# Turning x and B for a Mamba scan: transposing DMAs with GpSimd copies in place of TensorE transposes

## The chip, the cores and the metric

The kernel runs on one core of one Trainium2 chip. The metric is device time in microseconds, from the first to the last instruction of the launch and what lies around them; the median of three runs before the change is 1356.73 us (1356.61 to 1357.14).

The core has a matmul engine (TensorE, PE in the profile, its weight loads PEld), VectorE (DVE), ScalarE (ACT), GpSimd (POOL) and SyncE (SP), which here issues all DMAs.

## What is computed

A Mamba-2 layer, a residual sum with a layer norm, then a feed-forward layer with ternary weights and a second residual sum with a layer norm. The input is 2 sequences of 2048 tokens, 512 wide, in float32. Of the reference, the part that the change touches:

```python
zxbcdt = jnp.einsum('bld,ed->ble', u, W_in)
...
for k in range(D_CONV):
    xconv = xconv + xp[:, k:k + l, :] * conv_w[:, k]
xBC = jax.nn.silu(xconv)
x = xBC[..., :D_INNER].reshape(b, l, NHEADS, D_HEAD)
Bm = xBC[..., D_INNER:D_INNER + NGROUPS * D_STATE]
Cm = xBC[..., D_INNER + NGROUPS * D_STATE:]
...
Y_diag = jnp.einsum('bcshn,bczhn,bchsz,bczhp->bcshp', Ch, Bh, Lmat, xdt)
states = jnp.einsum('bczhn,bchz,bczhp->bchpn', Bh, decay_states, xdt)
...
Y_off = jnp.einsum('bcshn,bchpn,bchs->bcshp', Ch, prev_states, jnp.exp(cum))
y = (Y_diag + Y_off).reshape(b, l, h, p)
```

There are 8 heads of 128, one group of B and C with 64 states, and a state carried along each sequence.

## The kernel before

**Tiling and stages.** The first part goes over 16 groups of 256 tokens (`TG`), each of two chunks of 128 (`NC` = 2). `proj(g)` multiplies u (held as two float16 parts) by W_in: six pieces for z (L754) and nine blocks of 128 channels for x, B and C (L779), channels on partitions, tokens along the row. Block 8 holds B and C. On each block ScalarE applies one tap of the convolution as it reads PSUM (L792), VectorE the other three (L794), and ScalarE the silu (L798 for x, L809 and L811 for B and C).

The scan needs x and B with tokens on partitions. So TensorE transposes each block's two chunks of 128x128 float32 against `ident` into the PSUM bank `tr` (L802), and ScalarE copies the result into `xt` (L804). B's two pieces of 64x128 go the same way (L815, L817) into `bt`.

`steps(g)` computes dt and its running sum. The sum goes through DRAM (`cum_scratch`), so that it comes back as rows spread over all partitions (`cr`, `ec`; L873, L887), and VectorE subtracts and clips (L878). `scan(g, c)` handles one chunk: B^T C (L916) into the PSUM bank `ms`, masked (L917); the state's part of y (L930); the state's update, from B weighted (L934) and `xt` (L941, L948); the decay times dt times B^T C (L956) plus D on the diagonal (L958), multiplied by `xt` (L963); the gate (L965). Then a norm: a sum of squares (L970), a power on GpSimd (L972), and y in two float16 parts `yh` (L973) and `yl` (L975), which transposing DMAs turn into `th` and `tl` (L974, L976) for the output product with W_out (L983). ScalarE takes it out of PSUM (L986), and a DMA stores it in DRAM (L987).

Beside the groups the feed-forward weights are read, turned into ternary values (L1025 to L1027) and combined (L1032). The second part goes over 8 blocks of 512 tokens: a layer norm, seven products in place of eight for each of the three matrices (L1096, L1148), and the closing norm. It transposes its input by DMA too, as two float16 parts staged in `stg` (L1229).

**Order.** Every piece of work is an `op` of `Order`, with its engine, a cost, what it reads and writes, and a key from the list `KEYS`. `Order.run` goes through a planned time: on each engine it takes the ready `op` with the smallest key for which buffers are free, hands out the buffers and charges the `op`'s cost to its own engine alone. The order so found is emitted, and each engine then runs its own list strictly in that order; SP's list is its DMA queue, and an entry that waits holds up those behind it. GpSimd's list holds only small powers (L636, L696, L972, L1206, L1254) after the set-up.

**Buffers.** `tr` is one bank of PSUM, `ms` another. `xc` has four places of 256 columns, `xt` two of a whole group. `S` and `stg` (two of 2 KB each) and `us0` serve the feed-forward part alone. In `steps`, `scan` and the feed-forward part nothing but the names of this section is touched.

Of the kernel before, what the change touches and what calls it, by code (L numbers as in the profile page):

```python
# [12 lines left out]
F8 = mybir.dt.float8e4  # L13
AF = mybir.ActivationFunctionType
# [27 lines left out]
140 139 245 183 268 349 233 268 348 194 134 321 296 448 210 232 291 190 119 151 181 177 348 247 218 261 115 305 164  # L42
156 191 164 299 171 402 237 384 367 385 734 917 930 182 172 214 387 415 409 155 325 203 200 94 160 411 337 214 337
306 163 337 337 398 327 152 395 396 161 424 399 370 532 576 542 630 514 661 622 639 762 564 135 134 239 197 239 175
264 316 219 65 355 279 384 295 420 283 449 508 614 674 694 896 928 938 689 786 668 873 896 964 889 1242 891 879 920
999 856 952 1038 862 772 996 138 22 76 34 102 42 112 114 329 138 130 112 99 188 298 84 176 176 107 -9 160 159 116
228 128 172 210 252 211 348 304 268 316 448 420 282 390 703 399 394 474 429 430 431 395 523 337 463 372 462 456 506
687 744 752 824 727 794 786 782 88 348 349 169 216 212 185 465 437 664 529 411 520 533 514 508 544 572 535 552 573
594 574 575 512 592 592 684 540 600 745 640 687 606 625 698 681 289 225 340 448 309 142 340 370 436 348 176 190 353
303 273 175 379 282 662 640 695 696 597 682 778 667 200 316 294 129 255 19 205 231 602 626 650 607 735 517 783 670  # L50
369 283 422 447 626 339 450 353 549 385 632 679 549 255 600 642 617 779 763 660 708 652 712 701 264 514 514 538 827
520 575 638 528 653 736 692 226 314 489 471 146 173 56 172 214 182 117 630 408 305 608 674 535 671 685 738 681 720
717 1085 685 717 932 870 877 900 873 849 862 891 839 950 947 1129 940 946 975 1019 997 898 913 1088 936 1171 1438
989 989 1139 1105 997 437 344 217 489 494 615 643 593 586 512 384 223 402 421 480 368 470 638 782 725 786 797 739
827 999 1068 421 391 426 397 406 450 807 777 511 453 602 559 538 638 675 710 1142 1095 1194 1098 1113 1034 1154 1228
940 1055 950 984 1020 1098 1229 1360 984 1048 1193 967 973 1187 1224 1086 531 551 671 557 576 776 937 1032 889 894
1312 1249 1199 1067 797 830 563 573 764 795 790 827 876 878 839 1007 748 903 912 1329 1056 1066 1158 1072 981 1141
998 1103 1170 1206 1444 1395 529 563 797 869 796 778 793 855 882 844 861 839 924 829 830 913 924 908 912 980 935 949
1046 1060 993 1059 1066 966 1272 193 389 496 575 873 572 615 680 629 1188 938 1028 916 1051 1133 1161 872 1133 1225
1078 1364 1222 1382 1412 1405 1415 1480 1388 1472 1405 1454 1474 1368 1476 1560 1475 1499 1564 1415 1338 1504 1438  # L60
1394 1526 1636 1374 1214 1537 1818 1314 767 595 684 789 809 880 893 748 1006 1054 796 718 816 838 802 984 1082 1249
979 789 988 1060 920 1363 1338 1294 701 655 707 599 719 875 1052 986 836 875 884 954 973 1184 1031 1013 1034 1078
1065 1107 1189 1229 1079 1122 1066 1215 1085 1215 857 1204 1355 1433 1172 1198 1018 1265 1347 1277 1356 1530 614 658
733 656 649 699 835 939 1324 1361 928 872 1286 1397 1030 1049 949 1047 1156 1374 1354 1024 1410 1321 1413 1070 1400
1305 1414 1269 1291 1285 1291 1295 1478 1156 1426 1215 1403 1303 1441 1446 1439 1769 1394 866 991 1300 1389 1379
1436 1406 1368 1637 1239 1522 1397 1289 1278 1546 1392 1528 1790 1537 1618 1612 1259 1635 1357 1711 1648 1599 1996
1848 1240 1288 1412 1359 1425 1235 1428 1557 1445 1443 1380 1334 1574 1479 1520 1614 1624 1640 1871 1749 1972 2068
1842 1771 1752 1797 1815 1863 1829 1704 1917 1920 1807 1989 1852 2037 1664 2336 1769 1954 1996 1986 1920 1827 1994
1818 1746 1933 1887 1822 869 1331 1482 1499 1511 1601 1522 1496 1478 1709 1313 1514 1516 1516 1491 1564 1435 1675
1495 1702 1559 1609 1538 1847 1635 1608 1536 1737 1709 1709 1623 1827 1750 1929 1552 1749 1700 1656 1692 1974 1869  # L70
1918 1759 1949 1877 1875 1983 1875 1701 1913 1402 1735 1613 1553 1580 1673 1541 1764 1317 1624 1590 1516 1496 1614
1510 1621 1455 1699 1581 1324 1524 1689 1665 1798 2011 1967 1689 1808 1909 1873 1660 1905 1251 1309 1632 1626 1716
1572 1437 1581 1772 1690 1692 1665 1740 1664 1697 1679 1789 1550 1792 1718 1811 1747 1919 2171 1754 1870 1861 2146
2078 1142 1229 1681 1732 1920 1867 1880 1546 2129 1933 1964 1802 1940 1784 1812 1705 1962 2095 2094 1878 1958 1936
2031 1906 1961 2109 2118 1986 2525 1816 1668 1775 1706 1694 1981 1786 1974 1838 2093 1857 1906 2115 1910 2020 1866
1984 2047 2155 1960 2107 1921 2179 2123 1998 2150 2055 2086 2121 2075 2026 2123 1953 2053 2077 1979 2079 2327 2178
2162 2282 2376 2291 2472 2482 2308 2258 2103 2339 2344 1886 1735 1754 1933 1963 1960 1829 1888 2162 2209 1782 2008
2008 2049 1977 2311 2168 2061 1973 2081 1936 1949 1795 2227 2141 2162 1805 1998 2012 1797 1874 2141 1970 2023 1830
1908 1695 1888 1973 2186 1990 1932 2122 2067 2181 2052 2123 1999 2130 2127 1685 2023 1776 1892 1799 1900 1884 2028
2122 2253 2334 2339 2329 2055 2330 2304 1960 2014 1954 1918 1998 2119 2112 1971 2099 1992 2257 2154 2144 2273 2191  # L80
2156 1483 1637 1927 2118 2183 2206 2115 2057 1942 2171 2120 2216 2359 2036 2147 2040 2086 2181 2341 2192 2259 2268
2310 2489 2266 2369 2526 2438 2489 1689 1833 2030 2182 2257 2240 2194 2247 2498 2251 2150 2213 2309 2141 2170 2164
2351 2370 2327 2539 2485 2355 2460 2421 2457 2462 2448 2606 2785 2328 2087 2227 2195 2202 2320 2285 2305 2421 2198
2239 2384 2272 2296 2412 2263 2332 2203 2645 2223 2450 2405 2616 2457 2539 2774 2490 2613 2502 2585 2673 2676 2732
2752 2541 2462 2657 2714 2693 2933 2749 2911 2908 2518 2768 2820 2995 2645 2771 2889 2355 2276 2340 2475 2361 2370
2531 2413 2605 2533 2411 2199 2395 2619 2460 2468 2543 2587 2264 2325 2494 2403 2293 2455 2375 2488 2610 2488 2604
2680 2552 2614 2716 3088 2659 2488 2624 2622 2570 2876 2729 2797 2398 2445 2620 2354 2452 2575 2626 2697 2374 2577
2420 2458 2490 2316 2674 2906 2869 2734 2332 2532 2477 2752 2583 2749 2664 2615 2632 2681 2642 2874 2764 2925 3149
3124 3048 3154 3124 3092 3076 2931 1999 2139 2305 2593 2611 2521 2384 2454 2587 2474 2539 2681 2547 2479 2616 2516
2465 2692 2555 2745 2690 2694 2678 2803 2696 2873 2817 2764 3052 2216 2399 2423 2687 2704 2561 2711 2688 2895 2630  # L90
2598 2527 2807 2618 2560 2590 2549 2890 2726 2957 3025 3119 2945 2875 2907 2947 2915 3215 3424 2205 2544 2494 2403
2242 2393 2370 2730 2358 2828 2878 2725 2800 2911 2557 2863 2467 2834 2956 2899 3018 2820 2684 2608 2702 2797 2723
2784 2875 2884 3020 2942 2983 2915 2994 2938 3056 3163 3100 3053 3057 3280 3118 3484 3444 3266 3320 3221 3341 3430
3163 3101 2969 3134 3139 3269 3211 3132 3262 3338 2760 2710 2599 2661 2539 2813 3129 3048 3083 3125 2898 2982 2836
3056 3043 3099 2978 3118 2762 2775 2693 3117 3110 3184 2756 2965 2546 2636 2733 3367 3087 3195 2698 2895 2586 2635
2631 3039 3099 3136 3164 3232 3074 3254 3142 3341 3190 3293 3103 3068 3288 3069 3062 3095 3132 3112 2518 2457 2752
2477 2558 2722 3017 2999 2682 3140 3249 3245 3217 3137 3071 3016 2785 2599 2669 2780 2747 3099 2615 3052 3037 2827
2860 3068 3101 2745 2769 3080 3044 3166 3125 3060 3222 3235 3300 3265 3337 3297 3324 3464 3418 2672 2432 3081 2834
2916 3185 3134 3233 3384 3161 3160 3284 3280 2867 3017 3196 3213 3407 3280 3289 3365 3338 3394 3319 3419 3437 3421
# [225 lines left out]
class Slot:  # L325
# [5 lines left out]
    def view(self, shape, dtype):  # L331
        n = 1
        for s in shape[1:]:
            n *= s
        size = n * (1 if dtype == F8 else 2 if dtype == F16 else 4)
        assert size <= self.hi - self.lo
        a = self.tile[:shape[0], self.lo // 4:(self.lo + size) // 4]
        if dtype != F32:
# [973 lines left out]
```

## Time and profile before

| | us |
|---|---|
| median of three runs | 1356.73 |
| span of the profiled execution | 1355.1 |
| ACT evictions of x's transposes (L804), 128 | 47.9 busy, 374 ns each |
| ACT evictions of B's transposes (L817), 16 | 266 ns each (median) |
| PE transposes of x (L802), 256 | 50.2 busy, 278 ns each |
| PE products B^T C (L916), 64 records for 32 products | 15.3 busy |
| DVE taps (L794), 432 | 480 ns each (median) |
| POOL power for the norm (L972), 32 | 548 ns each (median) |
| SP transposing DMAs `th`, `tl` (L974, L976), 64 | 3.2 and 3.3 from issue to landing |
| SP transposing DMAs of the second part (L1229), 56 | 3.1 from issue to landing |

A float32 product is recorded as two matmuls where the program has one of them. "Busy" is the union of the instructions' spans; ends of matmuls are modelled and overlap the next one's start. "Idle before" in a group's line is the time for which the engine stood still just ahead of these instructions, and the name behind an arrow is what ended it. The last x transpose (L802) starts 732.9 us into the span, the last product that reads `xt` (L963) at 745.3, and the last output eviction of the first part (L986) at 766.2. The granted clock of TensorE is 0.998.

### The profile page before, as it was taken

What the parts mean: (1) busy time and instruction counts of PE and PEld (TensorE: products, weight loads), DVE (VectorE), ACT (ScalarE), POOL (GpSimd) and SP (SyncE); (2) the same over time, 40 slices, a digit from 0 to 9 for tenths busy, and PEclk for the clock granted to TensorE, in tenths of its full rate; (3) what the DMA queues carried; (4) which work ended last, traced back from release to release, by engine and by line L of the source; (5) the groups of instructions that cost most, each with busy time, mean ns of one, the idle gap of its engine ahead of it and who ended that gap; (6) DMA issues with size and microseconds to landing.
All of it is one profiled execution on the core that took longest, in us unless ns stands there. A gap on an engine that the chain in (4) does not pass through costs nothing.

```text
span 1355.1 us, 28913 instructions
## 1 busy us (share of the span) xinstructions
PE 1334.2 (98%) x11024; PEld 1057.9 (78%) x11024; DVE 1143.1 (84%) x3070; ACT 1041.0 (77%) x1996; POOL 80.4 (6%) x127
## 2 busy tenths in 40 slices
PE   9999999999999999999999999999999999999997
PEld 7777667766776677777676788888888888888886
DVE  5988878878999889889888697987979797979985
ACT  8888777768788778787767695969778695959772
POOL 1000000000000010000000000101010100001000
PEclk9999999999999999999999999999999999999999
DMA  6445666534543553573439530413222231314101
GB/s 242 139 116 147 171 164 165 147 111 124 155 137 99 156 139 80 137 185 85 112 76 247 127 63 9 125 24 110 40 79 55 94 56 60 82 40 102 32 17 47
DMA packets 194811, 145.60 MB, mean 107 GB/s; under 512 B 140656, under 2 KB 151920, under 8 KB 194672
## 3 DMA queue, kind: packets, MB, share of 16 engines
q1 hardware_dynamic: 194672, 143.75, 40.7%
q8 instruction: 86, 1.41, 0.4%
q14 instruction: 53, 0.43, 0.1%
HBM read 89.84 MB, written 22.41 MB: 83 GB/s over the span
## 4 chain that ended last, share of the span: by engine, by line
PE 66%; DVE 17%; ACT 10%; DMA 4%; issue 2%; POOL 0%; SPq 0%; POOLq 0%; ACTq 0%; DVEq 0%
PE sd L1096 9%; PE mm L779 9%; PE po L983 8%; PE mm L754 8%; PE po L1148 5%; PE sd L1148 4%; PE mm L1096 3%; PE po L1096 3%; PE sd L963 3%; DVE acc L794 3%; PE ms L1148 2%; DVE cr L956 2%; PE ms L1096 2%; PE mm L1148 2%; PE tr L802 2%
## 5 line engine op out<-in xcount | busy, mean ns | idle before, releaser
L1096 PEld LDWEIGHTS <-wx 128*128 128x128 fp8e4 x2048 | 200.2, 98 | 27.3 <-issue 2.9
L794 DVE SCALAR_TENSOR_TENSOR acc<-mm,cwu,acc 128x256 f32<-128x256 f32 x405 | 189.3, 479 | 21.6 <-ACT acc L792 19.2
L779 PEld LDWEIGHTS <-wx 128*128 128x128 f16 x1620 | 155.6, 97 | 33.2 <-issue 1.1
L1096 PEld LDWEIGHTS <-wz 128*128 128x128 fp8e4 x1536 | 150.2, 98 | 22.8 <-issue 4.6
L779 PE MATMUL mm<-uh,wx 128*128 128x260 f16 x1080 | 142.8, 274 | 0.7 <-DVE acc L794 0.5
L754 PE MATMUL mm<-wz,uh 128*128 128x344 f16 x720 | 119.9, 309 | 2.5 <-DVE acc L794 1.4
L983 PE MATMUL po<-wo,th 128*128 128x512 f16 x512 | 121.0, 379 | 0.3 <-ACT js L986 0.3
L792 ACT ACTIVATE acc<-mm,cst,cwu 128x256 f32<-128x256 f32 x135 | 74.8, 556 | 33.3 <-PE mm L779 31.8
L754 PEld LDWEIGHTS <-uh 128*128 128x128 f16 x720 | 68.5, 98 | 37.5 <-issue 4.4
L983 PEld LDWEIGHTS <-th 128*128 128x128 f16 x512 | 49.0, 98 | 49.5 <-issue 1.2
L779 PE MATMUL mm<-ul,wx 128*128 128x260 f16 x540 | 82.1, 273 | 0.0
L768 ACT ACTIVATE sz<-mm,szs 128x344 f32<-128x344 f32 (+1 forms) x90 | 48.4, 539 | 33.1 <-PE mm L754 28.4
L956 DVE SCALAR_TENSOR_TENSOR cr<-cr,dt,gm 128x128 f32<-128x128 f32 x256 | 72.1, 347 | 0.3
L798 ACT ACTIVATE xc<-acc 128x256 f32<-128x256 f32 x128 | 52.3, 412 | 25.5 <-DVE acc L794 25.1
L754 PE MATMUL mm<-wz,ul 128*128 128x344 f16 x360 | 67.2, 309 | 0.0
L963 PE MATMUL sd<-xt,cr 128*128 128x128 f32 x512 | 66.5, 277 | 0.1
L963 PEld LDWEIGHTS sd<-xt,cr 128*128 128x128 f32 x512 | 62.0, 192 | 3.1 <-issue 0.7
L983 PE MATMUL po<-wo,tl 128*128 128x512 f16 x256 | 60.5, 379 | 0.0
L878 DVE TENSOR_SCALAR cr<-cr,cum 128x128 f32<-128x128 f32 x256 | 54.0, 281 | 6.6 <-DMA cr<-cum_scratch 6.6
L804 ACT ACTIVATE xt<-tr 128x256 f32<-128x256 f32 x128 | 47.9, 374 | 11.7 <-PE tr L802 10.7
L1148 PEld LDWEIGHTS <-xt 128*128 128x128 f16 x512 | 50.1, 98 | 6.6 <-DVE xt L1131 0.9
L802 PE MATMUL tr<-ident,xc 128*128 128x128 f32 x256 | 50.2, 278 | 0.2
(356 smaller groups left out, 3275.1 us busy)
## 6 DMA issues: line engine op xcount, KB each, us to landing
cr<-cum_scratch SPq DMA_DIRECT2D x32, 512.0 KB, 5.6
ec<-cum_scratch SPq DMA_DIRECT2D x64, 128.0 KB, 5.5
fraw<-in_wupT_dram SPq DMA_DIRECT2D x32, 256.0 KB, 3.4
s_scratch<-js SPq DMA_DIRECT2D x32, 256.0 KB, 2.3
x<-s_scratch SPq DMA_DIRECT2D x32, 256.0 KB, 3.1
fraw<-in_wgateT_dram SPq DMA_DIRECT2D x32, 256.0 KB, 3.1
fraw<-in_wdownT_dram SPq DMA_DIRECT2D x32, 256.0 KB, 3.1
uraw<-in_uT_dram SPq DMA_DIRECT2D x15, 520.0 KB, 3.8
```

What stands on the lines that cost most here:

```text
L754: T.matmul(ps[:, :ZC], (uh, ul)[a][:, k, HL + c * P:HL + (c + 1) * P], wz4[b]()[:, j, k, :], start=(n == 0), stop=(n == 11))
L779: T.matmul(ps[:, :TW], wx4[a]()[:, j, k, :], (uh, ul)[b][:, k, :], start=(n == 0), stop=(n == 11))
L792: op(f"t{j}3", "S", act(TG, 2), lambda: S.activation(acc.ap, ps[:, HL:TW], AF.Identity, bias=cb[:, j:j + 1], scale=tap(3)), r=[ps, kc] + k ...
L794: op(f"t{j}{k}", "V", stt(TG), lambda k=k: V.scalar_tensor_tensor(acc.ap, ps[:, 1 + k:1 + k + TG], tap(k), acc.ap, ALU.mult, ALU.add), r=[ ...
L798: op(f"xs{j}", "S", silu(TG), lambda: S.activation(xc.ap, acc.ap, AF.Silu), r=[acc], w=[xc], table="silu")
L802: T.transpose(tr[:, c * P:(c + 1) * P], xc[:, c * P:(c + 1) * P], ident)
L878: V.tensor_scalar(cr[:, h, :], cr[:, h, :], cum[:, c * NH + h:c * NH + h + 1], 0.0, ALU.subtract, ALU.min)
L956: V.scalar_tensor_tensor(cr[:, h, :], cr[:, h, :], dt[:, c, h:h + 1], gm.ap, ALU.mult, ALU.mult)
L963: T.matmul(yp[hf][:, i * P:(i + 1) * P], cr[:, h, :], xt[:, c, h, :], start=is_first(g, c), stop=(is_first(g, c) or i == 3))
L983: T.matmul(po.ap, t[:, k, :], wo3[b]()[:, k, :], start=(q == 0 and k == 0), stop=(q == 2 and k == 7))
L1096: T.matmul(bank_[:, fi * TG:(fi + 1) * TG], wt[:, kt, f * P:(f + 1) * P], xT[i][:, a, :, kt, :], start=(first and fi == 0 and n == 0), sto ...
L1148: T.matmul(bank_[:, s_ * TG:(s_ + 1) * TG], X[k][j][:, a, e, s_ * P:(s_ + 1) * P], wt[:, k, :], start=(first and s_ == 0 and k == 0 and a ...
```

## The change

x and B are no longer turned by TensorE. ScalarE writes the silu of two neighbouring blocks into one `xc` (128 x 2 x 256 float32). GpSimd copies it as 16-bit words into `xst`, with all lower halves first and all upper halves behind them (`xi`, 2048 half words a partition). One transposing DMA turns the eight 128x128 tiles of half words into `xtt` (`xT`), and a second GpSimd copy joins the halves into float32 in `xt` (`xo`). A group has four of each. `xt` is now ordered by head, then chunk.

B is written by two activations, chunk 0 on partitions 0 to 63 and chunk 1 on 64 to 127, and goes the same way with 512 half words (`bi`, `bT`, `bo`), once a group. B^T C of both chunks is issued as one `op` of two products, whose operands lie on the two halves of the partitions, into two banks: `ms` takes over the bank `tr`.

The new staging buffers lie where `S`, `stg` and `us0` of the feed-forward part lie. Over the kernel TensorE has 288 transposes fewer, ScalarE 144 evictions fewer and 16 activations more, GpSimd 160 copies more, and SP 80 transposing DMAs more. All keys are new, and are read in hundredths instead of tenths, so the order of all work is another one, in the feed-forward part too. The planner's cost for a copy on GpSimd is `GC`.

```diff
--- before.py
+++ after.py
@@ -11,6 +11,7 @@
 F8 = mybir.dt.float8e4
+U16 = mybir.dt.uint16
 AF = mybir.ActivationFunctionType
...
 KEYS = """
-140 139 245 183 268 349 233 268 348 194 134 321 296 448 210 232 291 190 119 151 181 177 348 247 218 261 115 305 164
...
+-30479 132366 121996 -139138 53213 144054 145003 115337 159198 104723 -139139 129284 102640 122916 9708 125093
...
 """
@@ -332,7 +406,7 @@
...
-        size = n * (1 if dtype == F8 else 2 if dtype == F16 else 4)
+        size = n * (1 if dtype == F8 else 2 if dtype in (F16, U16) else 4)
@@ -409,7 +483,7 @@
...
-            o.key = int(k) / 10
+            o.key = int(k) / 100
@@ -586,9 +660,9 @@
...
-        for name, size, bufs in (("acc", 1024, 4), ("xc", 1024, 4), ("gq", 4096, 2)):
+        for name, size, bufs in (("acc", 1024, 4), ("xc", 2048, 2), ("gq", 4096, 2)):
             room(name, size, bufs, True)
-        for name, rest, parts in (("wo", 2048, (("wo", 8192, 2),)), ("BC", 0, (("B", 1024, 2), ("C", 1024, 2)))):
+        for name, rest, parts in (("wo", 2048, (("wo", 8192, 2),)), ("BC", 1024, (("B", 512, 2), ("C", 1024, 2)))):
@@ -598,10 +672,16 @@
...
-        for name, size, bufs in (("x1", 8192, 2), ("us0", 2048, 1), ("S", 2048, 2), ("stg", 2048, 2)):
-            room(name, size, bufs)
+        room("x1", 8192, 2)
+        room("us0", 2048, 1)
+        for name, first, size, bufs in (("S", "xst", 2048, 2), ("stg", "xtt", 2048, 2)):
+            host[name] = [pool.tile([P, size // 4], F32, name=f"{name}_{i}") for i in range(bufs)]
+            for nm in (first, name):
+                od.tag(nm, [Slot(t, 0, size) for t in host[name]])
+        for i, nm in enumerate(("bst", "btt")):
+            od.tag(nm, [Slot(host["us0"][0], (2 * i + k) * 512, 512) for k in range(2)])
         bank = [psum.tile([P, DM], F32, name=n) for n in ("mm0", "mm1", "tr", "sd0", "sd1", "sd2", "ms", "po")]
-        for name, bs in (("mm", (0, 1)), ("tr", (2,)), ("mx", (3, 4)), ("sd", (3, 4, 5)), ("ms", (6,)), ("po", (7,)),
+        for name, bs in (("mm", (0, 1)), ("mx", (3, 4)), ("sd", (3, 4, 5)), ("ms", (6, 2)), ("po", (7,)),
@@ -610,7 +690,7 @@
...
-                room(tag, size * (2 if dtype == F16 else 4), 2)
+                room(tag, size * (2 if dtype in (F16, U16) else 4), 2)
@@ -625,6 +705,7 @@
...
+        GC = lambda n: 0.15 + n * 1.9 / 1200.0
@@ -792,34 +873,36 @@
...
-                tr = mk("tr", [P, DM])
                 if j < 8:
-                    xc = mk("xc", [P, TG])
-                    op(f"xs{j}", "S", silu(TG), lambda: S.activation(xc.ap, acc.ap, AF.Silu), r=[acc], w=[xc], table="silu")
-
-                    def xtr():
-                        for c in range(NC):
-                            T.transpose(tr[:, c * P:(c + 1) * P], xc[:, c * P:(c + 1) * P], ident)
-                    op(f"xt{j}", "PE", 0.22, xtr, r=[xc], w=[tr])
-                    op(f"xe{j}", "S", act(TG), lambda: S.activation(d["xt"][:, :, j, :], tr[:, :TG].rearrange("p (c w) -> p c w", c=NC), AF.Copy), r=[tr], w=[(d["xt"], j)])
+                    if j % 2 == 0:
+                        d["xc"] = mk("xc", [P, 2, TG])
+                    xc, jp = d["xc"], j // 2
+                    op(f"xs{j}", "S", silu(TG), lambda: S.activation(xc[:, j % 2, :], acc.ap, AF.Silu), r=[acc], w=[(xc, j % 2)], table="silu")
+                    if j % 2:
+                        st, tt_, xt = mk("xst", [P, 2, 2 * TG], U16), mk("xtt", [P, 2, 2 * TG], U16), d["xt"]
+                        op(f"xi{jp}", "G", GC(4 * TG), lambda: G.tensor_copy(st.ap, xc.ap.rearrange("p j n -> p (j n)").bitcast(U16).rearrange("p (n e) -> p e n", e=2)), r=[xc], w=[st])
+                        op(f"xT{jp}", "SP", 1.25, lambda: nc.sync.dma_start_transpose(
+                            out=tt_.ap.rearrange("p e (r q) -> p (e r) q", q=P), in_=st.ap.rearrange("p e n -> p (e n)")), r=[st], w=[tt_], kb=330)
+                        op(f"xo{jp}", "G", GC(4 * TG), lambda: G.tensor_copy(
+                            xt[:, 2 * jp:2 * jp + 2].rearrange("p j c q -> p (j c q)").bitcast(U16).rearrange("p (n e) -> p e n", e=2), tt_.ap), r=[tt_], w=[(xt, jp)])
                 else:
-                    B = d["B"] = mk("B", [64, TG])
+                    B = d["B"] = mk("B", [P, P])
...
-                    op("bs", "S", 0.42, lambda: S.activation(B.ap, acc[0:64, :], AF.Silu), r=[acc], w=[B], table="silu")
+                    for c in range(NC):
+                        op(f"bs{c}", "S", silu(P), lambda c=c: S.activation(B[c * 64:c * 64 + 64, :], acc[0:64, c * P:(c + 1) * P], AF.Silu), r=[acc], w=[(B, c)], table="silu")
...
-
-                    def btr():
-                        for c in range(NC):
-                            T.transpose(tr[:, c * 64:(c + 1) * 64], B[:, c * P:(c + 1) * P], ident[:64, :64])
-                    op("btr", "PE", 0.25, btr, r=[B], w=[tr])
-                    op("bte", "S", act(P), lambda: S.activation(bt.ap, tr[:, :P].rearrange("p (c w) -> p c w", c=NC), AF.Copy), r=[tr], w=[bt])
+                    bst, btt = mk("bst", [P, 2, P], U16), mk("btt", [P, 2, P], U16)
+                    op("bi", "G", GC(TG), lambda: G.tensor_copy(bst.ap, B.ap.bitcast(U16).rearrange("p (n e) -> p e n", e=2)), r=[B], w=[bst])
+                    op("bT", "SP", 1.25, lambda: nc.sync.dma_start_transpose(out=btt.ap, in_=bst.ap.rearrange("p e n -> p (e n)")), r=[bst], w=[btt], kb=100)
+                    op("bo", "G", GC(TG), lambda: G.tensor_copy(
+                        bt.ap.rearrange("p c n -> p (c n)").bitcast(U16).rearrange("p (n e) -> p e n", e=2), btt.ap), r=[btt], w=[bt])
...
-            d["xt"] = mk("xt", [P, NC, NH, P])
+            d["xt"] = mk("xt", [P, NH, NC, P])
@@ -911,9 +994,14 @@
...
-            gps = mk("ms", [P, DM])
-            gm = mk("gm", [P, P])
-            o("gps", "PE", 0.45, lambda: T.matmul(gps[:, :P], B[:, cs], C[0:64, cs], start=True, stop=True), r=[B, C], w=[gps])
+            if c == 0:
+                d["gps"] = [mk("ms", [P, DM]) for _ in range(NC)]
+
+                def gmm(gp=d["gps"]):
+                    for i in range(NC):
+                        T.matmul(gp[i][:, :P], B[rows(i), :], C[rows(i), i * P:(i + 1) * P], start=True, stop=True)
+                o("gps", "PE", 0.5, gmm, r=[B, C], w=d["gps"])
+            gps, gm = d["gps"][c], mk("gm", [P, P])
@@ -938,7 +1026,7 @@
...
-                            T.matmul(sp[rows(hf), i * P:(i + 1) * P], bw[:, hf * 4 + i, :], xt[:, c, hf * 4 + i, :], start=True, stop=True)
+                            T.matmul(sp[rows(hf), i * P:(i + 1) * P], bw[:, hf * 4 + i, :], xt[:, hf * 4 + i, c, :], start=True, stop=True)
@@ -960,7 +1048,7 @@
...
-                        T.matmul(yp[hf][:, i * P:(i + 1) * P], cr[:, h, :], xt[:, c, h, :], start=is_first(g, c), stop=(is_first(g, c) or i == 3))
+                        T.matmul(yp[hf][:, i * P:(i + 1) * P], cr[:, h, :], xt[:, h, c, :], start=is_first(g, c), stop=(is_first(g, c) or i == 3))
...
```

## The prediction

> **What bounds the kernel now.** I read first the page's busy times and the chain of waits, then the stage in which the edit lies, then TensorE's timeline around one transpose.
>
> ```profile
> PE 1334.2 (98%) x11024; PEld 1057.9 (78%) x11024; DVE 1143.1 (84%) x3070; ACT 1041.0 (77%) x1996; POOL 80.4 (6%) x127
> PE 66%; DVE 17%; ACT 10%; DMA 4%; issue 2%; POOL 0%; SPq 0%; POOLq 0%; ACTq 0%; DVEq 0%
> ```
>
> TensorE is nearly full, and the chain lies on it for two thirds; VectorE comes second in both. Next, busy time by stage (columns: stretch, PE, PEld, DVE, ACT, POOL, clock, DMA share, GB/s): the middle of the first part, and the feed-forward part, whose instructions the edit leaves as they are.
>
> ```profile
> 92.00:690.00 598.00, 594.51 (x4604) 423.75 (x4604) 510.96 (x1633) 466.04 (x889) 27.26 (x39) 1.00 0.52 136
> 736.00:1355.00 619.00, 605.99 (x5480) 534.50 (x5479) 516.22 (x1070) 459.28 (x880) 41.28 (x62) 1.00 0.28 67
> ```
>
> In the first part VectorE is busy 510.96/598 = 85.4%, and TensorE hardly idles. One group's length: the second output eviction (L986) of group 0 starts at 115.7, that of group 15 at 766.2, so (766.2 - 115.7)/15 = 43.4 us. VectorE works 0.854 x 43.4 = 37.1 us of it and has 6.3 to spare.
>
> A busy TensorE row overstates one short instruction, since ends are modelled. Start to start tells what a transpose takes from the stream:
>
> ```profile
> 301.78 0.75 PE L754 MATMUL mm<-wz,ul 128*128 128x344 f16 x4
> 302.36 0.38 PE L802 MATMUL tr<-ident,xc 128*128 128x128 f32 x2
> 302.58 1.06 PE L779 MATMUL mm<-uh,wx 128*128 128x260 f16 x8
> ```
>
> The pair takes 302.58 - 302.36 = 0.22 us, not 0.38; over all 128 pairs the median is 0.218.
>
> **What is removed.** TensorE: 128 pairs for x at 0.218 = 27.9 us, and 16 pairs for B at 0.238 (the same reading, L815) = 3.8. B^T C (L916) stands now as two products, 0.11 to 0.21 apart start to start; as a pair on separate row halves one may hide behind the other: 16 x 0.11 to 0.21 = 1.8 to 3.4, of which I take 2.3. Together 34 us in 16 groups, 2.1 a group: 41.3 us if TensorE goes on setting the pace. ScalarE loses 128 evictions of 0.374 and 16 of 0.266, 52 us, and gains 16 activations (one for B becomes two). It stands at 77% and not on the path, so I count nothing; if its cover fails that is a gain already limited by TensorE.
>
> **What is added to GpSimd.** 128 copies of 2048 half words a partition and 32 of 512. No such copy is in this trace. The nearest rows:
>
> ```profile
> masks.py:199 POOL TENSOR_SCALAR_AFFINE_SELECT ident<-ident 128x128 f32<-128x128 f32 x1 | 0.3, 292 | 0.1
> masks.py:197 POOL MEMSET ident<- 128x128 f32 x1 | 0.2, 204 | 0.3 <-POOLq L1302 0.3
> L1302 POOL MEMSET const-bfloat16-1.0<- 128x1 bf16 x1 | 0.1, 102 | 0.0
> ```
>
> From one element to 128 the memset grows by 102 ns, 0.80 ns an element; the affine select, if it starts from the same 102, by 1.50. So the large copy takes 1.75 to 3.16 us and the small one 0.51 to 0.87. A copy has no arithmetic and is nearest to the memset: I take 1.75 and 0.51. A group then has 8 x 1.75 + 2 x 0.51 = 15.0 us of copies, and GpSimd is free for that (27 us busy in 598).
>
> **What the copies do to VectorE** decides the case. GpSimd's small powers show that the two engines get in each other's way. Alone a power takes 0.55 us:
>
> ```profile
> 165.96 0.69 DVE L925 TENSOR_TENSOR ec<-ec,BC 128x512 f32<-128x512 f32 x1
> 166.05 1.00 POOL L636 TENSOR_TENSOR iu<-sc,half 128x1 f32<-128x1 f32 x1 [24.03 <-DVE q L850]
> ...
> 505.83 1.28 DVE L975 SCALAR_TENSOR_TENSOR yl<-y,rs,yh 128x1024 f16<-128x1024 f32 x1
> 505.99 1.52 POOL L636 TENSOR_TENSOR iu<-sc,half 128x1 f32<-128x1 f32 x1 [4.65 <-DVE sc L635]
> ...
> 240.62 0.55 POOL L636 TENSOR_TENSOR iu<-sc,half 128x1 f32<-128x1 f32 x1 [12.89 <-DVE dec L924]
> 240.66 0.70 DVE L925 TENSOR_TENSOR ec<-ec,BC 128x512 f32<-128x512 f32 x1
> ```
>
> Where a VectorE instruction with two SBUF inputs was already running, the power ended 0.40 us after that instruction's end (166.65 to 167.05; 507.11 to 507.51): GpSimd waited for all of it. Beside instructions that read PSUM (L794, L965) powers kept 0.55. In the third pair the power came first, and VectorE lost at most 0.01 us; but a power reads one element, a copy 2048. So the bounds of what a copy takes from VectorE are nothing, and all of the copy's time in which a two-SBUF instruction is due. I take the second, because in the one direction that the rows show the wait is for the whole instruction.
>
> How often one is due: instructions with two SBUF inputs (L956, L958, L975, L925, L934, L735, the ternary L1026 and L1032, which held up powers too, and small ones) fill 262 of the 600 us from 100 to 700. Going along VectorE's timeline there, a 1.75 us copy at evenly spread starts meets the start of the next such instruction early enough to hold it for 0.95 us on average; a 0.51 us copy for 0.17. A group loses 8 x 0.95 + 2 x 0.17 = 7.9 us. VectorE then needs 37.1 + 7.9 = 45.0 us a group, more than today's 43.4. The order cannot allow for it: the planner's list charges a copy to GpSimd alone.
>
> The Trainium skill, "SBUF — State Buffer", section "Who interferes with whom", speaks against this change: a VectorE instruction with two SBUF inputs contends with a GpSimd instruction that reads SBUF, and whichever issues first holds the shared port to its end. That agrees with the 1.00 and 1.52 us powers; for the other direction no row here shows it. By that rule the sum is the one with 7.9 us a group; by the third pair alone it would be 0.
>
> **What is added to SP and the DMA engines.** 64 transposing DMAs of the size of those of L1229 (1.23 us of queue, 3.1 us to landing) and 16 of a quarter. SP issues for 264 of the 600 us from 100 to 700; 80 x 1.23 = 98 us over 700 lift that from 44% to 58%. The DMA share of 0.52 rises with 4.25 transposes beside the group's present four, so there is room. Behind a transpose that waits for its copy stand the row loads (cr, ec), u, and th, tl; on GpSimd the powers, and so yh, th and the output products, stand behind a joining copy that waits for a landing. I count these at nothing while VectorE is the one late: the order issues x's steps well ahead of their readers. Without that cover see the third rival. One chain is longer: copy 1.75, transpose 1.2 + 3.1, copy 1.75 = 7.8 us in place of some 0.6. It matters at the end of the first part, where the last transpose (732.9) lies 12 us ahead of the last product that reads x (745.3): nothing, and at most 7 us.
>
> **Forecast.** VectorE sets the pace of 16 groups. At 100% busy a group is 45.0, +1.6 each, +26 us; at the 43.98/46 = 95.6% of its fullest stretch of this part (506 to 552) 47.1, +3.7, +59. The middle is +42: 1355.1 + 42 = 1397, and the median of the runs stands 1.6 above the span: 1399. Its own range is 1375 to 1440 (the long chain and denser conflicts once VectorE never idles are in its upper end).
>
> **Rivals.**
> 1. VectorE loses next to nothing, because the copies' reads leave gaps as the power's did, or because its 20 us a group of other work fill the waits. Then TensorE keeps the pace: 1355.1 - 34 + 1.6 = 1323, with VectorE at 37.1/41.3 = 90%; each microsecond lost beyond some 2 a group goes into the time, so 1320 to 1345. For it: TensorE's two thirds of the chain, the third pair. Against: the whole-instruction waits, and only 6.3 us spare. It decides if a copy costs VectorE under about 0.5 us. Chance 0.35.
> 2. Half the loss: gain and loss cancel, 1354 to 1359. It needs some 0.7 us a copy. Chance 0.04.
> 3. Not the port but GpSimd's queue: a joining copy waits for its landing with a power behind it, 3.1 + 1.75 = 4.9 us once a group, and the output products come that much late: 16 x 4.9 - 34 = +44, 1401. For it: the queue runs in order and the powers are needed at once. Against: GpSimd's 60% of free time. Chance 0.10.
> 4. Copies at the affine select's pace, 3.16 us, by the same count 2.06 us lost for each large copy and 0.36 for each small one, 17.2 a group: 54.3 us a group, +174, 1531. Chance 0.05.
>
> The forecast itself has 0.46. About 0.2% is what a measurement of this kernel can tell from no change. Faster 0.35, within 0.2% 0.04, slower 0.61 (0.46 + 0.10 + 0.05). The range takes in most of rival 1 and leaves out rival 4: 1324 to 1445.
>
> **What would show it.** Right: VectorE's two-SBUF instructions (L956, L958, L975) grow beside the copies or start late with GpSimd as releaser, the L794 ones stay at 0.48; VectorE over 95% in the first part, TensorE with idle stretches ended by VectorE; the feed-forward part as long as before. Copies near 1.75 us, start to start, where nothing holds them; longer records include waits for VectorE. Wrong: VectorE's mean durations unchanged and TensorE still over 98% busy in a first part some 34 us shorter (rival 1), or powers that start late behind copies waiting for a DMA (rival 3). The forecast falls if copies prove clearly shorter than 1.75 us, or if VectorE's extra stays under 4 us a group.

## The result, and the profile after

The changed kernel takes 1423.2 us (median of four runs, 1421.54 to 1424.79) against 1356.93 for the one before on the same chip (four runs, 1356.61 to 1358.53): 1.0487 times as long, interval 1.0473 to 1.0502, or +66 us. The profiled execution spans 1419.8 us.

The page's busy times and its chain of waits, as they were shown of before:

```profile
PE 1316.2 (93%) x10736; PEld 1027.3 (72%) x10736; DVE 1212.2 (85%) x3070; ACT 1018.6 (72%) x1876; POOL 277.3 (20%) x287
PE 38%; DVE 37%; ACT 15%; issue 5%; DMA 4%; POOL 1%; SPq 1%; POOLq 0%; ACTq 0%; DVEq 0%
```

TensorE loses 18 us of work and falls from 98% to 93%. Its share of the chain falls from 66% to 38%, and VectorE's rises from 17% to 37%. By stage (stretch, PE, PEld, DVE, ACT, POOL, clock, DMA share, GB/s):

```profile
92.00:690.00 598.00, 537.76 (x4099) 372.14 (x4097) 531.76 (x1524) 416.31 (x740) 169.68 (x161) 0.99 0.65 151
```

In the same 598 us TensorE now stands still for 60 us where it had 3.5. VectorE has gone from 510.96 to 531.76 us, 88.9%: it is not full. The first part's last output eviction starts at 830.6 instead of 766.2, and from there to the end of the span it is 589 us in both kernels. So all of the loss lies in the first part. The first group's second eviction comes at 125.6 instead of 115.7, 10 us late already, and the groups behind it take (830.6 - 125.6)/15 = 47.0 us each instead of 43.4.

The two longest entries among TensorE's waits (total us, times, longest us), and then the longest of the kernel before:

```profile
PE mm L860 <- DVE acc L875: 24.7, 21, 4.4
PE mm L835 <- DVE acc L875: 17.5, 15, 3.3
```

```profile
PE mm L754 <- DVE acc L794: 1.4, 4, 0.5
```

The convolution's taps (L875, which is L794 of before) free the PSUM bank into which the next projection goes. The taps are not slower; they start later. The groups (line, engine, operation, tiles, shapes, count | busy us, mean ns | idle before, and what ended it) tell who is slower:

```profile
L875 DVE SCALAR_TENSOR_TENSOR acc<-mm,cwu,acc 128x256 f32<-128x256 f32 x405 | 188.8, 475 | 16.3 <-ACT acc L873 13.2
...
L886 POOL COPY xt<-stg 128x1024 uint16<-128x1024 uint16 x64 | 92.0, 1440 | 109.9 <-DMA stg<-S 98.6 <-PE sd L1029 3.5 <-PE mm L860 2.9
L1044 DVE SCALAR_TENSOR_TENSOR cr<-cr,dt,gm 128x128 f32<-128x128 f32 x256 | 83.9, 388 | 0.4
L883 POOL COPY S<-xc 128x1024 uint16<-128x1024 uint16 x64 | 78.5, 1227 | 227.4 <-ACT xc L880 216.5 <-issue 5.7 <-DMA stg<-S 4.9
...
L961 DVE TENSOR_SCALAR cr<-cr,cum 128x128 f32<-128x128 f32 x256 | 60.8, 306 | 7.7 <-DMA cr<-cum_scratch 7.6
...
L935 DVE SCALAR_TENSOR_TENSOR q<-q,w 128x16 f32<-128x16 f32 x112 | 29.6, 265 | 0.8
...
L817 DVE TENSOR_SCALAR szs<-iw,iu 128x3 f32<-128x3 f32 x15 | 6.0, 401 | 0.3 <-POOL iu L717 0.3
```

Two things are to be seen. First, `xt<-stg` and `S<-xc` (staging is printed under the name of the tile it shares) have 1024 elements a partition, and those of B 256. The 2048 and 512 half words given above for these copies are twice too many: two blocks of 256 float32 are 512 words. A splitting copy takes 1.05 us and a joining one 1.34 (medians; the shortest 1.03 and 1.33), for B 0.46 and 0.48 (the shortest 0.40 and 0.47). Secondly, the instructions whose inputs lie in SBUF, the core's own memory, are longer, while the taps, which have an input in PSUM, the banks that TensorE writes, are not (479 ns before). The same four groups of the kernel before:

```profile
L956 DVE SCALAR_TENSOR_TENSOR cr<-cr,dt,gm 128x128 f32<-128x128 f32 x256 | 72.1, 347 | 0.3
L878 DVE TENSOR_SCALAR cr<-cr,cum 128x128 f32<-128x128 f32 x256 | 54.0, 281 | 6.6 <-DMA cr<-cum_scratch 6.6
...
L852 DVE SCALAR_TENSOR_TENSOR q<-q,w 128x16 f32<-128x16 f32 x112 | 19.2, 171 | 0.3
...
L736 DVE TENSOR_SCALAR szs<-iw,iu 128x3 f32<-128x3 f32 x15 | 3.3, 219 | 0.0
```

So 347 ns became 388, 281 became 306, 171 became 265, 219 became 401. In the timeline one sees it happen (start, us from the first start to the last end, engine, line, operation, tiles):

```profile
326.76 2.03 DVE L961 TENSOR_SCALAR cr<-cr,cum 128x128 f32<-128x128 f32 x4
327.04 1.33 POOL L886 COPY xt<-stg 128x1024 uint16<-128x1024 uint16 x1
```

Four of these tensor_scalar (one tensor read from SBUF) take 0.87 us before the change:

```profile
308.32 0.87 DVE L878 TENSOR_SCALAR cr<-cr,cum 128x128 f32<-128x128 f32 x4
```

Here the copy runs at its own 1.33, and the four take 2.03.

### The profile page after: what moved, and what is told of

Its sections match the earlier page's. It is cut to its first block, busy times and chain, and to the rows that moved or that the text cites. A ratio compares the mean times of both kernels' runs of the same rounds, so it can differ in the third digit from the quotient of the medians.

```text
span 1419.8 us, 28668 instructions
## 1 busy us (share of the span) xinstructions
PE 1316.2 (93%) x10736; PEld 1027.3 (72%) x10736; DVE 1212.2 (85%) x3070; ACT 1018.6 (72%) x1876; POOL 277.3 (20%) x287
## 4 chain that ended last, share of the span: by engine, by line
PE 38%; DVE 37%; ACT 15%; issue 5%; DMA 4%; POOL 1%; SPq 1%; POOLq 0%; ACTq 0%; DVEq 0%
DVE acc L875 7%; PE sd L1236 7%; PE sd L1184 6%; DVE cr L1044 4%; PE po L1184 3%; PE mm L1184 3%; PE mm L860 3%; PE mm L1236 3%; PE mm L835 3%; DVE cr L961 2%; PE po L1071 2%; PE po L1236 2%; DVE y L1053 2%; DVE cr L1046 2%; DVE gq L1120 2%
## 5 line engine op out<-in xcount | busy, mean ns | idle before, releaser
L875 DVE SCALAR_TENSOR_TENSOR acc<-mm,cwu,acc 128x256 f32<-128x256 f32 x405 | 188.8, 475 | 16.3 <-ACT acc L873 13.2
L883 POOL COPY S<-xc 128x1024 uint16<-128x1024 uint16 x64 | 78.5, 1227 | 227.4 <-ACT xc L880 216.5
L886 POOL COPY xt<-stg 128x1024 uint16<-128x1024 uint16 x64 | 92.0, 1440 | 109.9 <-DMA stg<-S 98.6
L1342 POOL TENSOR_TENSOR lnr<-lnr,mhalf 128x1 f32<-128x1 f32 x32 | 27.8, 869 | 417.0 <-DVE lnr L1279 379.5
L1044 DVE SCALAR_TENSOR_TENSOR cr<-cr,dt,gm 128x128 f32<-128x128 f32 x256 | 83.9, 388 | 0.4
L961 DVE TENSOR_SCALAR cr<-cr,cum 128x128 f32<-128x128 f32 x256 | 60.8, 306 | 7.7 <-DMA cr<-cum_scratch 7.6
```

Of the source, the lines that this page charges most:

```text
L875: op(f"t{j}{k}", "V", stt(TG), lambda k=k: V.scalar_tensor_tensor(acc.ap, ps[:, 1 + k:1 + k + TG], tap(k), acc.ap, ALU.mult, ALU.add), r=[ ...
L883: op(f"xi{jp}", "G", GC(4 * TG), lambda: G.tensor_copy(st.ap, xc.ap.rearrange("p j n -> p (j n)").bitcast(U16).rearrange("p (n e) -> p e n ...
L886: op(f"xo{jp}", "G", GC(4 * TG), lambda: G.tensor_copy(xt[:, 2 * jp:2 * jp + 2].rearrange("p j c q -> p (j c q)").bitcast(U16).rearrange(" ...
L961: V.tensor_scalar(cr[:, h, :], cr[:, h, :], cum[:, c * NH + h:c * NH + h + 1], 0.0, ALU.subtract, ALU.min)
L1044: V.scalar_tensor_tensor(cr[:, h, :], cr[:, h, :], dt[:, c, h:h + 1], gm.ap, ALU.mult, ALU.mult)
```

## The experiments

Times are medians, and a ratio is to the kernel before on the same chip. Three chips were used, and the kernel before takes 1356.9 to 1358.0 us on them, so a difference of 1 us between two runs is not to be told from nothing. The edits are shown shortened. The lines of one kernel can lie a few numbers off those of another.

### E1, E2: how much of a copy's length counts, and is it its reading?

E1 is the changed kernel with copies of 8 half words a partition in place of 1024 and 256. Staging is cleared once at the start, so that the scan gets but a few columns of x and B; in E1, E2, E6 and E8 this adds 4.0 us to VectorE's work, at the very start, where it otherwise waits. The expectations call E1 the sliver run.

```diff
-G.tensor_copy(st.ap, <xc as halves>)
+G.tensor_copy(st[:, :, 0:4], <xc as halves>[:, :, 0:4])   # xo, bi, bo likewise
```

E2 is E1 with the rest of each copy's destination written by a memset on GpSimd: it stays busy, though less long than in the changed kernel (for `xt` a memset takes 0.52 us, the copy 1.34), and reads next to nothing. What is computed is as in E1.

```diff
+G.memset(st[:, :, 4:], 0)   # after each short copy; xo, bi, bo likewise
```

> The changed kernel, same order, same transposing DMAs and waits, but each GpSimd copy moves 8 half words a partition instead of 1024 (x) or 256 (B), so most of x and B is left out; staging buffers are cleared once at the start. Port theory (the copies' reads hold VectorE's second SBUF input for as long as they run): the 62 us that VectorE's instructions grew by go away, so 1423 falls to 1361 or below, and to 1323 if the whole gain of TensorE's lost transposes then shows; VectorE's two-input instructions are back at 347, 171 and 281 ns. Queue theory (powers and x late behind GpSimd's in-order copies and their landings): also a fall, since the copies are short, but by less, 1380 to 1400, as the landings stay. Order theory (the new order or the longer chain through DMA costs it): stays above 1400.

> As the sliver run, and behind each sliver copy GpSimd clears the rest of the destination (a memset that writes 2 KB or 0.5 KB a partition and reads nothing), so that GpSimd is busy about as long as with the copies. Port theory, if only reads are in VectorE's way: within 15 us of the sliver run, with VectorE's two-input rows at their old length and perhaps the tensor_scalar rows still long. Queue theory: within 20 us of the changed kernel, 1403 to 1443. Order theory: no change from the sliver run, both above 1400.

E1 took 1375.59 us, ratio 1.0129 [1.0112, 1.0147]. E2 took 1376.45, 1.014 [1.0125, 1.0155]. The groups of E2:

```profile
L888 POOL MEMSET S<- 128x1016 uint16 x64 | 60.5, 945 | 0.0
...
L1047 DVE SCALAR_TENSOR_TENSOR cr<-cr,dt,gm 128x128 f32<-128x128 f32 x256 | 71.8, 342 | 0.3
L964 DVE TENSOR_SCALAR cr<-cr,cum 128x128 f32<-128x128 f32 x256 | 57.4, 313 | 4.3 <-DMA cr<-cum_scratch 4.2
...
L938 DVE SCALAR_TENSOR_TENSOR q<-q,w 128x16 f32<-128x16 f32 x112 | 18.4, 165 | 0.8
...
L822 DVE TENSOR_SCALAR szs<-iw,iu 128x3 f32<-128x3 f32 x15 | 6.2, 411 | 0.3 <-ACT fraw L1098 0.3
```

The bulk of the copies costs 1423.2 - 1375.6 = 47.6 us, most of the +66. It isn't GpSimd's being busy, nor its queue: E2's GpSimd works 144 of the 598 us of the middle stretch (170 in the changed kernel, 64 in E1), and the time is E1's within 1 us. It is what the copies read. Without the reading, the instructions with two SBUF inputs are as short as in the kernel before (342 and 165 ns, against 388 and 265 with the copies). Those with one SBUF input, the tensor_scalar, are held by writes too (313 and 411 ns; E1 has 279 and 219). The sum of the durations of all VectorE instructions agrees: 1360 us in E1, 1384 in E2, 1418 in the changed kernel. Without the 4 us of clearing that E1 has and the changed kernel has not, the copies' bulk lengthened them by 62 us. E2's 24 us are almost all in instructions with one SBUF input (8.8 in L964); why they cost no time was not looked into, but they show that a longer instruction on VectorE need not make the kernel longer. E1 does not come down to the time of before, though: some 19 us are not in the copies' length.

### E3: the copies alone, in the kernel before

E3 is the kernel before plus, in each of its first 14 groups, eight copies of 1024 half words and two of 256 on GpSimd, from `xt` and `bt` into staging that nobody reads. Order, transposes and evictions stay.

```diff
+G.tensor_copy(<S or stg as halves>, <two heads of xt as halves>)   # after xe1 to xe7
```

> The kernel before, its order and its TensorE transposes, with 8 GpSimd copies of 1024 half words and 2 of 256 added to each of the first 14 groups, behind the evictions that they read; nothing reads what they write. Port theory: VectorE grows by 14/16 of 62 = 54 us there; it had 6.3 us a group to spare, so between a third and all of it is seen: 1375 to 1412. Queue theory: only powers that wait behind a copy cost, 1357 to 1372. Order theory: 1357 within 3.

E3 took 1417.75 us, ratio 1.0443 [1.0428, 1.0459]: +60 in 14 groups, 4.3 a group. Its groups and its chain:

```profile
L979 DVE SCALAR_TENSOR_TENSOR cr<-cr,dt,gm 128x128 f32<-128x128 f32 x256 | 78.9, 368 | 0.3
...
L875 DVE SCALAR_TENSOR_TENSOR q<-q,w 128x16 f32<-128x16 f32 x112 | 30.3, 270 | 0.3
```

```profile
PE 47%; DVE 35%; ACT 10%; issue 4%; DMA 3%; POOL 1%; SPq 0%; POOLq 0%; ACTq 0%; DVEq 0%
```

With order and other work as before, the copies lengthen the same instructions and put VectorE on the chain. All VectorE durations together grow by 58.4 us (1367.0 to 1425.4, 1.2 of it clearing), and the time by 60, more than the 1412 that was expected at most: here VectorE's 6.3 spare microseconds a group absorb nothing. GpSimd's queue has a small part in it: the norm's 32 powers start a mean of 309 ns behind VectorE's result instead of 83, 7 us over all of them. That each hold falls ahead of something due next in a list run strictly in order, while the free time lies elsewhere in the group, is the likely reading; it was not traced.

### E4, E4b: what TensorE's transposes are worth

The reverse: the kernel before with its transposes cut to 4 rows and 4 columns (E4), and then left out (E4b). The evictions stay and read a bank that was cleared, so x and B are zero for the scan, in E4 but for four columns of each piece.

```diff
-T.transpose(tr[:, c * P:(c + 1) * P], xc[:, c * P:(c + 1) * P], ident)
+T.transpose(tr[:, c * P:c * P + 4], xc[0:4, c * P:(c + 1) * P], ident[:4, :4])   # E4
+xtr = lambda: None                                                                 # E4b, btr likewise
```

> The kernel before, its order, evictions and waits, with TensorE's transposes of x and B cut to 4 columns, so most of x and B is left out: what TensorE's share of the gain is worth in the old order. If TensorE sets the pace there, as the start-to-start rows say: 128 x 0.2 + 16 x 0.2 = 29 us less, 1328, and 1325 to 1340. If VectorE or the chain through it already sets the pace and TensorE only fills in: above 1347.

> The kernel before with no TensorE transposes of x and B at all (the run that cut them to 4 columns and 4 rows still spent 0.22 us of the stream on each pair, so it took nothing away); ScalarE's evictions stay and read a bank cleared once, so x and B are left out of the scan. If TensorE sets the old kernel's pace: 128 x 0.218 + 16 x 0.238 = 32 us less, 1320 to 1335. If the order and the chain through VectorE and ScalarE set it, 1345 or more; then the prediction's 34 us were never to be had by removing TensorE's work alone.

E4 took 1362.76 us, ratio 1.0038 [1.0025, 1.0051]. It took nothing away, as TensorE's timeline shows:

```profile
301.00 0.75 PE L756 MATMUL mm<-wz,ul 128*128 128x344 f16 x4
301.67 0.28 PE L804 MATMUL tr<-ident,xc 4*128 4x4 f32 x2
301.89 1.34 PE L756 MATMUL mm<-wz,uh 128*128 128x344 f16 x8
```

The 4x4 pair still takes 301.89 - 301.67 = 0.22 us start to start. So E4 tells nothing of their worth; why it is 5 us longer stays open.

E4b took 1353.46 us (ten runs), ratio 0.9971 [0.996, 0.9982]: all 144 pairs, 32 us by their starts, are worth 3.5. TensorE still shows 97% busy, yet in the stretch from 92 to 690 us it stands still for 25.7 us (572.33 busy of 598) where it had 3.5. VectorE's taps are the longest entries among TensorE's waits over the span:

```profile
PE mm L756 <- DVE acc L796: 6.3, 8, 1.6
PE mm L781 <- DVE acc L796: 5.8, 13, 0.9
```

TensorE did not set the pace alone; 98% busy said little of what a microsecond less on it brings.

### E5, E7, E9: can the copies be kept out of VectorE's way?

E5 moves the splitting copies to ScalarE, which the change had relieved of 52 us of evictions, and E7 all of the copies. E9 leaves them on GpSimd, each large one in four pieces of 256 half words.

```diff
-G.tensor_copy(st.ap, <xc as halves>)
+S.activation(st.ap, <xc as halves>, AF.Copy)                        # E5: xi, bi; E7: xo, bo too
+[G.tensor_copy(st[:, :, k * 128:(k + 1) * 128], ...) for k in range(4)]   # E9: xi, xo
```

> The changed kernel, same order, with the splitting copies (x and B) on ScalarE instead of GpSimd; the joining ones stay. Port theory: what stays on GpSimd is 64 x 1.33 and 16 x 0.47 of 64 x (1.04 + 1.33) and 16 x (0.40 + 0.47) us, 56% of the hold, so 1376 + 0.56 x 48 = 1403 if ScalarE's extra 64 us (64 x 1.0, nearest the 1.05 us pass over 1024 elements) hide in its idle 30%; 1395 to 1415. Queue theory: no less than 1415, since the chain is as long.

> The changed kernel, same order, with all 160 copies on ScalarE, none on GpSimd. Port theory: VectorE's two-input rows are back at their old length (347, 171, 281 ns); ScalarE carries some 64 x 2 x 1.0 + 32 x 0.3 = 138 us more, 88% of the middle stretch, and delays evictions: 1376 if that hides, 1420 if half of it is seen; 1380 to 1410. If the port were not what costs, it would be slower than the changed kernel, above 1430.

> The changed kernel, each of the 128 large copies cut into four of 256 half words, the same words in all. Port theory with a hold for a whole instruction: one hold lasts 0.3 to 0.4 us instead of 1.04 to 1.33, VectorE gets in between, its longest 128x128 two-input instruction falls from 1417 ns to below 800, and its growth of 58 us over the sliver run by a third to two thirds: 1385 to 1410. If GpSimd holds the port across back-to-back copies, or if GpSimd's own time counts: 1420 or more.

E5 took 1423.82 us, ratio 1.0495 [1.0477, 1.0514]; E7 1444.42, 1.0646 [1.0628, 1.0664]. E7's chain, and one of its groups:

```profile
PE 38%; ACT 32%; DVE 19%; DMA 5%; issue 5%; SPq 1%; POOL 1%; POOLq 0%; ACTq 0%; DVEq 0%
```

```profile
L1044 DVE SCALAR_TENSOR_TENSOR cr<-cr,dt,gm 128x128 f32<-128x128 f32 x256 | 72.0, 344 | 0.4
```

In E7 VectorE gets back its 344 ns, and its durations sum to 1360 us, 58 below the changed kernel's. But ScalarE's share of the chain goes from 15% to 32%, with 514 of the 598 us busy; the copies last as long on it as on GpSimd (1.05 and 1.34 us) and take 167 us of it instead of the 138 expected. What VectorE no longer loses, ScalarE does, in a list whose order was found for copies on GpSimd. E7 was expected at 1380 to 1410, and a time above 1430 was to speak against the hold on VectorE. It does not, since VectorE's rows are short again; but E7's time says nothing for the hold either. E5 was expected at 1395 to 1415: VectorE's durations fall by 22 us to 1396, ScalarE works 462 of the 598 us instead of 416, and the time stays. Only these two placements were tried, with that order kept.

E9 took 1400.75 us, ratio 1.0328 [1.031, 1.0346], 22.5 less than the changed kernel, though GpSimd is busy longer. Lines by shape (minimum/median/maximum ns, first and last start):

```profile
L1043 DVE SCALAR_TENSOR_TENSOR cr<-cr,dt,gm x256: 251/345/591, 79.6 to 768.4; 128x128 f32<-128x128 f32 x128
```

The longest of these now takes 591 ns instead of 1417 in the changed kernel. So a held instruction waits for the rest of one copy and not of several, and a shorter copy has less of it. VectorE's durations sum to 1401.5 us, 17 below the changed kernel's.

### E6, E8: what is left without the copies

E6 is E1 without the 80 transposing DMAs. E8 is the changed kernel without copies and without those DMAs: the work of before less transposes and evictions, in the new order. In both the scan gets no x and no B.

```diff
-op(f"xT{jp}", "SP", 1.25, lambda: nc.sync.dma_start_transpose(...), ...)
+op(f"xT{jp}", "SP", 1.25, lambda: None, ...)   # bT too; in E8 also xi, xo, bi, bo
```

> The sliver run without its 80 transposing DMAs, so x and B are left out: GpSimd's joining sliver waits for the splitting one only. Where the sliver run's other 18 us over the kernel before come from: if from the transposes (landing of 3.1 us, SP's queue, DMA share 0.69), 1320 to 1350; if from the new order of the engines' lists, 1365 to 1378, as the sliver run.

> The changed kernel with none of its 160 copies and none of its 80 transposing DMAs: x and B are left out of the scan, and what is left is the new order with the work that both kernels share, ScalarE without the 144 evictions. The run without TensorE's transposes in the old order took 1353. If the slivers and their handshakes made the 10 us between that kind of kernel and 1367: 1350 to 1358. If the new order of the lists itself is slower: 1362 to 1368.

E6 took 1367.34 us, ratio 1.0077 [1.0062, 1.0092]; E8 1366.37, 1.0068 [1.0053, 1.0083]. So the transposing DMAs cost some 8 (E1 less E6; 7 by the ratios), the short copies with their waits nothing clear of noise (1.0), and E8 is 13 us slower than E4b, which also has no turning of x and B and runs the old order. The output evictions (L1076 of E8, L984 of E4b, by line as above):

```profile
L1076 ACT ACTIVATE js<-po,osc x32: 664/678/689, 109.9 to 775.6; 128x512 f32<-128x512 f32 x32
```

```profile
L984 ACT ACTIVATE js<-po,osc x32: 665/684/690, 102.9 to 764.9; 128x512 f32<-128x512 f32 x32
```

The new order is 7 us behind at the first eviction. At the end of group 11 it is level (611.8 and 611.4), and in the last four groups it falls 11 behind (775.6 against 764.9). That it is the order and not the work rests on this comparison: E8 even has 144 evictions fewer than E4b. It also has B^T C as a pair, other buffers and a lower granted clock (0.995 against 0.998), which were not tried apart.

## Why the prediction was right, and where its sum was not

The direction, the mechanism and the range held. The +42 that was forecast came from terms of which several were wrong in opposite directions, so that the time lay as near to it as it did is in part luck. What the runs show, each step taken away in turn:

| step | us | from |
|---|---|---|
| transposes off TensorE, old order | -3.5 | E4b less before |
| new order with its pair and buffers, 144 evictions fewer | +13 | E8 less E4b |
| short copies and their waits | +1, not clear of noise | E6 less E8 |
| transposing DMAs | +8 | E1 less E6 |
| the copies' bulk | +48 | changed kernel less E1 |
| sum | +66 | |

- **The copies hold VectorE: shown.** E1 and E3 show it from both sides, E2 that for instructions with two SBUF inputs it is what the copies read, and E9 that a hold lasts for the rest of one copy. The taps, which read PSUM, were not held, and the second part stayed as long as it was, as expected.
- **Size of the hold: mis-sized.** The half words were counted double. With 1024 and 256 the memset's row gives 0.92 and 0.31 us and the affine select's 1.63 and 0.48; measured were 1.05 and 1.34, 0.46 and 0.48, inside those bounds. The prediction's own averaging, with the shorter copies, gives 4.8 us a group instead of 7.9; VectorE's instructions grew by 62/16 = 3.9. With 4.8 the forecast's own rule gives 41.9 us a group at a full VectorE and 43.8 at 95.6%: 24 us less to 7 us more than before, and not +42. Here lies the luck: the double count stood in for the terms below that were put at nothing. By the condition that the prediction set itself (copies clearly shorter than 1.75 us, under 4 us a group) its forecast falls as a sum, but the time was not rival 1's for that.
- **"VectorE sets the pace at 95 to 100%": failed.** It was 88.9% busy. On a VectorE that sets the pace its 6.3 spare microseconds a group would have paid first. Instead 62 us of longer instructions cost 47.6, in E3 58.4 cost 60, and in E2 24 cost 1, so the sum alone does not give the time. TensorE's waits for the taps fit a hold that delays a tap, the tap a bank, the bank TensorE.
- **TensorE's 34 us: failed.** They are not in the forecast's +42, but made rival 1's 1323 and rival 3's 1401. In the old order the 32 of them that are transposes were worth 3.5. Busy shares and a chain that lies on TensorE for two thirds did not show that VectorE's taps would be late right behind it, as E4b's waits do.
- **Order, transposing DMAs at nothing: failed,** by 13 and 8. The DMA share (0.52, then 0.65) had room, and the transfers cost time all the same. `th` and `tl` land in 3.6 and 4.1 us in E1 and in 3.3 and 3.7 in E6; whether that is how they cost it was not traced.
- **ScalarE's 52 us at nothing: not shown apart.** E8 has the relief together with the new order and is still longer than before; E5 and E7 show that its free time is not free for copies either.
- **Rival 3, GpSimd's queue: refuted.** E2 fills GpSimd at a cost of 1 us, and the norm's powers start a mean of 256 ns behind VectorE's result instead of 83 (147 in E8, without any copy) and 1.34 us at most, where the rival needed 4.9 a group.
- **L878 left out of the held instructions: wrong.** A power had kept its 0.55 us beside it, yet the copies hold it (281 to 306 ns). The Trainium skill, "SBUF — State Buffer", section "Who interferes with whom", says more than the prediction took from it: that tensor_scalar and copies can contend as well, and that an instruction with two SBUF inputs contends with a GpSimd instruction that reads, not with one that only writes. E2's rows agree on both: tensor_scalar at 411 ns under writes, two-input instructions at 165.

No run ended below both kernels; E4b, which leaves out work, is the only one below before. An order searched with the holds charged to VectorE was not tried, and why this order loses 13 us, beyond where, stays open.

## What to carry to other kernels

Charge a GpSimd copy to VectorE too: here instructions with two SBUF inputs, and tensor_scalar as well, waited for the end of a copy during which they became due. Four short pieces cost 22 us less than one long one, and VectorE's free share, 15%, was no cover for the holds of E3. Price the removal of work by removing it (E4b), not by its busy time: 32 us of TensorE were worth 3.5. Measure a new order by itself, without the work it was made for, before its gain or loss is put down to that work.

## What had not been expected of the hardware

- A float32 transpose pair takes the same 0.22 us start to start at 4x4 as at 128x128 (E4).
- The two products of B^T C in the changed kernel, on the two halves of the partitions and into two banks, run side by side, as the prediction had hoped: they start 0.01 us apart.

```profile
329.00 0.37 PE L1002 MATMUL tr<-BC 64*128 64x128 f32 x1
329.01 0.37 PE L1002 MATMUL ms<-BC 64*128 64x128 f32 x1
```

- The granted clock was lower in some stretches in which TensorE idled. In the changed kernel's stretch from 460 to 506 us (columns as in the stages above) it is 0.93, and 1.00 in the next:

```profile
460.00:506.00 46.00, 38.81 (x248) 24.74 (x248) 39.47 (x113) 33.40 (x58) 11.34 (x10) 0.93 0.63 155
506.00:552.00 46.00, 40.65 (x321) 28.59 (x320) 40.42 (x109) 31.56 (x53) 16.04 (x13) 1.00 0.67 154
```

The first 92 us of E8 and of E4b differ in the same way, 79.56 us busy at 0.96 and 87.68 at 1.00. The busy time alone does not tell it: from 368 to 414 us TensorE is busy for 38.91 us, and the clock is 1.00. How much of the time this is was not measured. An estimate from the mean granted clocks, 0.998 before and 0.989 in the changed kernel's four runs, bounds it at some 13 of the 66 us, were TensorE on the path throughout; in E1, at 0.9925, the same bound is 8, so some 5 of the copies' 48 us can be clock.
